# Gate products in 64-row pairs, a 128-row pass for the sines, whole gate blocks in chosen slots, keys four slots ahead

## Chip, cores and metric

The program runs on one core of one Trainium2 chip. The core has five engines with instruction queues of their own: TensorE for matrix products (PE in the profile, its weight loads shown apart as PEld), VectorE (DVE), ScalarE (ACT), GpSimd (POOL) and SyncE (SP, which here only issues DMAs). The metric is the device time of one execution in microseconds (us). Lower is better. Before the change it is 2940.25 us, the median of three runs (2938.42 to 2941.7).

## What is computed

The reference is a block of two layers over x of 8 x 512 x 256 (batch, tokens, width) and a context of the same shape: cross-attention, a feed-forward part, a second cross-attention, a second feed-forward part. Only the first cross-attention is touched. It has 16 heads of 64, and every attention weight is multiplied by a gate that depends on the two tokens' boxes:

```python
delta_x = log(clip(abs((cx_q - cx_k) / w_q), 0.001, None))    # delta_y alike
delta_w = log(w_q / w_k)                                      # delta_h alike
mul = (100.0 * stack([delta_x, delta_y, delta_w, delta_h]))[..., None] * [1, 1000 ** -0.5]
emb = concatenate([sin(mul), cos(mul)])                       # 16 numbers for a pair of tokens
g   = relu(einsum('bnmd,hd->bhnm', emb, Wg) + bg)             # 16 numbers -> 16 heads
a   = q @ k.T / sqrt(64)
mn  = softmax(log(clip(g, 1e-6, None)) + a)
out = (mn @ v) @ Wo.T + bo
```

The softmax over log g + a is computed as g times exp(a), divided by its own sum. All arithmetic is float32.

## The kernel before

**Stages.** First a stage projects keys, values and queries of the eight batches to device memory and prepares the boxes (about the first 356 us). Then comes the loop of the gated cross-attention, to about 1960 us, and after it the attention across the batch, the routed experts and the second layer (the rest). The change lies in the loop and in what the first stage prepares for it.

**The loop.** There are 32 steps (`NSTEP`), one for each batch and each tile of 128 queries. A step has eight slots `p`, one for each pair of heads. In slot `p` of step `i` PE does, in this order: the scores of pair p+1 (`scores`, L469: two products that use 64 rows each, one per head, in two PSUM banks), a piece of the next step's gates (`gate_half`, L449), the eight transposes of the exponentials of pair p (`weigh`, L485), a second piece, the products of pair p-1 with the values (`values`, L505), and in some slots a third piece, the transposes of the output (`outputs`, L527, slots 1, 3, 5, 7) or the output projection (`mix`, L536, slot 2). DVE takes the row maxima of the scores (L473), multiplies the transposed exponentials by the gates (L487) and divides by the sums (L511, L513). ACT takes the exponentials (L476). The order on PE, ACT and DVE is the order of the code (`MANUAL`)[...]. The order of the DMAs on SP is chosen by the scheduler.

**The gates.** For the x and y differences each query has its own sines and cosines over the keys. For width and height the sine of a difference of logs falls apart into products of a query's and a key's numbers, so eight rows (`qx`, `kx`) serve all queries, and a ninth carries the bias. A block of 13 queries (`QB`) so needs 4 x 13 rows of sines, 9 shared rows and 4 x 13 rows of cosines: 116 rows of PE (`GR`), sines from row 0, cosines from row 64. The weights `emb` (116 rows x 128 keys) are loaded, the table `wst` (116 rows x 13 queries x 16 heads) is streamed, and the result has keys as rows. Ten blocks (`NB`) times four groups of 128 keys make 40 products a step. A half block is two key groups in one PSUM bank of 2 x 208 columns; two such banks alternate (tag `g`, `bufs=2`). Each half is copied to the gate tile by one instruction (L455), on DVE in slots 0, 2 and 7, on ACT in the others: 9 and 11 copies a step. The number of halves for each slot is `HALVES`.

**The sines' numbers.** `lt` and `nt` hold 5 passes of 512 keys (`NP`): rows 0 to 51 and 64 to 115 are two blocks of queries. For a step two or three ahead the loop runs `offsets` (DVE, L324, slots 4 and 5), `sizes` (ACT, absolute value, L330, slot 5), `clip` (DVE, slot 6), `log` (ACT, slot 7), `turns` (DVE, next step's slot 0), `whole` and `rest` (DVE, slot 1), `rest_sizes` (DVE) and `sines` (ACT, twice, L352 and L353, slot 2). Four DMAs (`place`, L361, slot 3) then bring `lt` and `nt` to their rows of `emb`. `lt` may be written again by `offsets` once its DMAs have landed.

**Loads.** SP fetches one pair's keys three slots ahead (`load_key`, L419, 3 buffers) and values two ahead (`load_value`, L425, 3 buffers). PSUM [...]: scores 2, transposes 2, gates 2, outputs 2.

## Time and profile before

| what | value |
|---|---|
| median of three runs | 2940.25 us |
| the profiled execution | 2940.68 us |
| its span, first to last instruction | 2938.9 us |
| mean granted TensorE clock | 0.987 of full |
| one step of the loop, mix to mix | 49.75 us, 32 steps |
| DVE busy in a step | 37.4 us |
| ACT busy in a step | 30.3 us |
| DMA in the loop | about 150 GB/s, 0.55 of the 16 engines' time |

The profile has a page with a busy time for each engine, groups of equal instructions with their mean duration, and a timeline. In a timeline line the first number is the start, the second the length of the merged stretch, and "x8" the number of instructions in it. Float32 products go through PE in two passes, and each pass is an instruction of its own in the trace with a weight load in front of it; so 40 gate products are 80 passes. A transpose is one pass. Ends of PE instructions are modelled, so distances between starts are used for PE, not durations.

### The profile page before, as it was taken

The numbers are of one execution on the slowest core, as the hardware profiler recorded it, in microseconds if no ns is written. First come the engines' busy times: TensorE is split into PE (matmuls) and PEld (weight loads), VectorE is DVE, ScalarE is ACT, GpSimd is POOL, SyncE is SP. The second block draws the span as 40 slices with busy tenths as digits, with TensorE's granted clock in tenths as the row PEclk, the third lists the DMA queues.
The fourth block names the chain that finished last, engine by engine and source line by source line (L and its number), as shares of the span: only waits on it lengthen the run. The fifth ranks groups of instructions, "written<-read, shape, count | busy, mean of one in ns | idle before, by whom it ended". The sixth has DMA issues, their size and how long they took to land.

```text
span 2938.9 us, 39143 instructions
## 1 busy us (share of the span) xinstructions
PE 2866.8 (98%) x15188; PEld 2095.2 (71%) x15188; DVE 1826.5 (62%) x2862; ACT 1404.0 (48%) x2196; POOL 138.4 (5%) x138
## 2 busy tenths in 40 slices
PE   8999999999999999999999999999999998999998
PEld 3444478888888888888888888877775665456566
DVE  6432177777777777777777767557862112566757
ACT  4332256566666666656565665435541121343434
POOL 2000000000000000000000000000002111212100
PEclk9999999999999999999999999999998998999999
DMA  7775545555555555454546464443113333111100
GB/s 226 220 227 188 180 119 155 142 155 142 150 152 146 156 140 158 135 163 131 166 131 167 131 166 129 134 128 140 47 55 129 129 127 107 58 44 57 29 15 22
DMA packets 270105, 381.84 MB, mean 130 GB/s; under 512 B 55048, under 2 KB 136840, under 8 KB 267104
## 3 DMA queue, kind: packets, MB, share of 16 engines
q1 hardware_dynamic: 266848, 370.95, 43.9%
q0 software_dynamic: 3072, 8.39, 1.0%
q8 instruction: 120, 1.97, 0.3%
q14 instruction: 65, 0.53, 0.1%
HBM read 237.23 MB, written 73.88 MB: 106 GB/s over the span
## 4 chain that ended last, share of the span: by engine, by line
PE 79%; DVE 13%; issue 2%; DMA 2%; ACT 1%; SPq 0%; POOL 0%; ACTq 0%; DVEq 0%; POOLq 0%
PE pg L449 13%; PE po L505 11%; PE pS L469 7%; PE pT L485 6%; PE pk L226 6%; PE ph L1525 4%; PE pw L536 4%; PE ph L1308 4%; PE py L1317 4%; PE py L1540 4%; PE pv L241 3%; DVE nm L473 2%; PE pz L1497 2%; DVE lt L346 2%; PE pq L700 2%
## 5 line engine op out<-in xcount | busy, mean ns | idle before, releaser
L476 ACT ACTIVATE e<-pS,nm 128x512 f32<-128x512 f32 x512 | 324.3, 684 | 576.4 <-DVE nm L473 576.0
L449 PE MATMUL pg<-wst,emb 116*128 116x208 f32 (+1 forms) x2560 | 581.5, 350 | 8.1 <-DVE gate L455 5.8
L449 PEld LDWEIGHTS pg<-wst,emb 116*128 116x128 f32 x2560 | 414.1, 189 | 205.2 <-issue 79.8
L505 PEld LDWEIGHTS po<-v,at 128*128 128x128 f32 x4096 | 493.0, 192 | 0.1
L505 PE MATMUL po<-v,at 128*128 128x65 f32 x4096 | 485.7, 272 | 0.0
L473 DVE TENSOR_REDUCE nm<-pS 128x2 f32<-128x1024 f32 x256 | 312.5, 1221 | 176.2 <-PE pS L469 176.2
L487 DVE SCALAR_TENSOR_TENSOR at<-gate,pT 128x1024 f32<-128x1024 f32 x256 | 311.1, 1215 | 46.4 <-PE pT L485 45.4
L469 PE MATMUL pS<-kT,qT 64*128 64x512 f32 x1024 | 291.2, 641 | 5.6 <-ACT e L476 2.0
L485 PE MATMUL pT<-ident,e 128*128 128x128 f32 x2048 | 266.4, 273 | 0.0
L485 PEld LDWEIGHTS pT<-ident,e 128*128 128x128 f32 x2048 | 239.8, 141 | 13.9 <-DVE o L513 1.5
L455 DVE COPY gate<-pg 128x416 f32<-128x416 f32 (+1 forms) x289 | 164.6, 570 | 51.2 <-PE pg L449 30.9
L455 ACT COPY gate<-pg 128x416 f32<-128x416 f32 x351 | 166.7, 531 | 33.6 <-PE pg L449 31.2
L1321 DVE TENSOR_TENSOR ye<-py,b 128x256 f32<-128x256 f32 x32 | 13.6, 424 | 208.0 <-PE py L1317 208.0
L1312 ACT ACTIVATE hT<-ph,eb 128x512 f32<-128x512 f32 x64 | 44.0, 687 | 177.7 <-PE ph L1308 171.9
L226 PE MATMUL pk<-ctxT,wk__121 128*128 128x512 f32 x256 | 114.9, 604 | 11.2 <-DMA ctxT<-in_ctxT 7.6
L63 POOL TENSOR_TENSOR ln_rs<-ln_ve,mhalf 128x4 f32<-128x4 f32 (+1 forms) x25 | 25.5, 1019 | 2050.5 <-DVE ln_ve L62 1990.3
L1525 PE MATMUL ph<-xnT,wf 128*128 128x512 f32 (+2 forms) x320 | 118.7, 513 | 1.8 <-ACT xnT L1393 1.5
L536 PE MATMUL pw<-wo,oT 128*128 128x256 f32 x512 | 117.6, 383 | 0.5 <-ACT oT L528 0.5
L241 PE MATMUL pv<-wv,ctxT 128*128 128x512 f32 x256 | 114.7, 593 | 1.0 <-DVE vs L245 1.0
L1308 PE MATMUL ph<-dT,w 128*128 128x512 f32 x256 | 111.9, 595 | 2.7 <-DVE dT L1293 2.1
L469 PEld LDWEIGHTS pS<-kT,qT 64*128 64x128 f32 x1024 | 77.8, 184 | 51.1 <-issue 36.4
L226 PE MATMUL pk<-xnT,wq 128*128 128x512 f32 x256 | 113.0, 594 | 0.6 <-DVE xnT L261 0.6
(252 smaller groups left out, 3910.7 us busy)
## 6 DMA issues: line engine op xcount, KB each, us to landing
v<-vdr SPq DMA_DIRECT2D x256, 260.0 KB
kT<-kdr SPq DMA_DIRECT2D x256, 256.0 KB
emb<-lt SPq DMA_DIRECT2D x64, 520.0 KB
emb<-nt SPq DMA_DIRECT2D x64, 520.0 KB
vdr<-vs SPq DMA_DIRECT2D x8, 2080.0 KB
kdr<-st SPq DMA_DIRECT2D x64, 256.0 KB
qdr<-st SPq DMA_DIRECT2D x64, 256.0 KB
qT<-qdr SPq DMA_DIRECT2D x32, 512.0 KB
```

The source lines that it names most:

```text
L226: nc.tensor.matmul(pk, w[:, c, m * P : (m + 1) * P], src[:, c, :], start=(c == 0), stop=(c == 1))
L449: nc.tensor.matmul(pg[:, c, 0 : nq * H], embs[i % 2][R, blk // 2, blk % 2, kc * P : (kc + 1) * P], wst[i % 2][R, q0 * H : (q0 + nq) * H], ...
L455: copy(gates[i][:, :, 2 * hf : 2 * hf + 2, q0 : q0 + nq].rearrange("p h k q -> p k h q"), pg[:, :, 0 : nq * H].rearrange("p k (q h) -> p k ...
L469: nc.tensor.matmul(pS[:, t, :], qTs[i][rows, p, :], kT[rows, :], start=True, stop=True)
L473: nc.vector.tensor_reduce(nm, pS, AX.X, ALU.max, negate=True)
L476: nc.scalar.activation(e[:, t, :], pS[:, t, :], AF.Exp, bias=nm[:, t : t + 1])
L485: nc.tensor.transpose(pT[:, t, kc, :], e[:, t, kc * P : (kc + 1) * P], ident)
L487: nc.vector.scalar_tensor_tensor(at, gates[i][:, 2 * p : 2 * p + 2], 1e-6, pT, ALU.max, ALU.mult)
L505: nc.tensor.matmul(po[:, 2 * (p % 2) + t, :], at[:, t, kc, :], v[:, kc, t, :], start=(kc == 0), stop=(kc == NQ - 1),)
L536: nc.tensor.matmul(pw, oT[:, c, :], wo[:, c, :], start=(c == 0), stop=(c == PAIRS - 1))
L1308: nc.tensor.matmul(ph, w1[:, c, f * P : (f + 1) * P], dT[:, c, :], start=(c == 0), stop=(c == 1),)
L1525: nc.tensor.matmul(ph[:, 0:n], wf[:, c, f * P : (f + 1) * P], xnT[:, c, tok], start=(c == 0), stop=(c == 1),)
```

## The change

- **Blocks.** The 128 queries of a step are split into two halves of 64 (`HQ`). A block has 6 queries of each half (`QB`), 4 x 6 sines, 4 x 6 cosines and 9 shared rows: 57 rows (`GR`), one half at row 0 and the other at row 64. There are 11 blocks; the last has 4 queries of each half. A product has 57 rows and 96 columns (64 in the last block). `gate_block` issues eight products: for each of four key groups one from rows 0 to 56 and one from rows 64 to 120, into two PSUM banks (tags `g0` and `g1`, one buffer each). Each bank is then copied by one instruction.
- **Slots.** Every slot starts with one block, ahead of the scores. Slots 0, 1 and 5 have a second block between the scores and `weigh`. `BLOCKS` says which engine copies each of the two banks ("A" for ACT, "V" for DVE): 12 copies on ACT and 10 on DVE a step.
- **Sines' numbers.** The rows of `lt` and `nt` are packed without gaps: five groups of 24 rows and one of 8, 128 rows in all, with 4 passes of 512 keys. `offsets` is whole in slot 4, `sizes` in slot 5, `clip` and `log` in slot 6, `turns` in slot 7, `whole` in slot 0, `rest` in slot 1. `place` has ten DMAs for `lt` (slot 3) and ten for `nt` (slot 4). `load_products` and `load_keys` have more DMAs with fewer rows each.
- **Keys** are loaded four slots ahead into four buffers.
- In the first stage `wst` has 128 rows of 64 queries in place of 116 rows of 128, and the steps prepared there follow the new layout.

```diff
-QB = 13
-NB = 10
-GR = 64 + 4 * QB
+HQ = P // 2
+QB = 6
+NB = 11
+GR = 8 * QB + 9
+NS = P // (4 * QB)
...
-        def place(j):
-
-            for src, r0 in ((lt, 0), (nt, 64)):
-                for half in range(2):
+        def place(j, *trig):
+
+            for c in trig or (0, 1):
+                src, r0 = (lt, nt)[c], 4 * QB * c
+                for s in range(NS):
+                    rows = src[4 * QB * s : 4 * QB * (s + 1)]
+                    for g in (s // 2,) if s < 4 else (0, 1):
+                        b0, n = (4 * (s % 2), 4) if s < 4 else (8, 2)
+                        nc.sync.dma_start(
+                            out=embs[j % 2][64 * g + r0 : 64 * g + r0 + 4 * QB, b0 : b0 + n, :],
+                            in_=rows[:, 0:4, :] if s < 4 else rows[:, 2 * g : 2 * g + 2, :],
+                        )
+                for t in range(4):
+                    at = 64 * (t // 2) + r0 + 8 * (t % 2)
                     nc.sync.dma_start(
-                        out=embs[j % 2][r0 : r0 + 4 * QB, :, half, :],
-                        in_=src[64 * half : 64 * half + 4 * QB],
+                        out=embs[j % 2][at : at + 8, NB - 1, :], in_=src[4 * QB * NS :, t, :]
                     )
...
-                kTs[i, p] = wk.tile([P, S], F32, name="kT", tag="kT", bufs=3)
+                kTs[i, p] = wk.tile([P, S], F32, name="kT", tag="kT", bufs=4)
...
+        def gate_block(i, blk, engines="AV"):
...
+            if i == 0 and blk % 2:
+                pT = ps.tile([P, 2, NQ, P], F32, name="pT", tag="t")
+                pgs = [pT[:, g] for g in range(2)]
+            else:
+                pgs = [ps.tile([P, NQ, P], F32, name=f"pg{g}", tag=f"g{g}") for g in range(2)]
+            for kc in range(NQ):
+                for g in range(2):
+                    rows = slice(64 * g, 64 * g + GR)
+                    nc.tensor.matmul(
+                        pgs[g][:, kc, 0 : nq * H],
+                        embs[i % 2][rows, blk, kc * P : (kc + 1) * P],
+                        wst[i % 2][rows, q0 * H : (q0 + nq) * H],
+                        start=True, stop=True,
+                    )
+            for g in range(2):
+                q = HQ * g + q0
+                copy = nc.scalar.copy if engines[g] == "A" else nc.vector.tensor_copy
+                copy(
+                    gates[i][:, :, :, q : q + nq].rearrange("p h k q -> p k h q"),
+                    pgs[g][:, :, 0 : nq * H].rearrange("p k (q h) -> p k h q", h=H),
+                )
...
+        BLOCKS = (("AA", "AV"), ("AA", "AV"), ("AV",), ("VV",), ("AV",), ("AA", "AV"), ("AV",), ("VV",))
...
-                    load_key(i, p + 3)
+                    load_key(i, p + 4)
+                    gate_block(i + 1, next(blocks), BLOCKS[p][0])
                     scores(i, p + 1)
-                    if p == SINES:
+                    if p == 2:
                         features(i + 2, rest_sizes, sines)
-                    if p == LOG:
-                        features(i + 3, log)
-                    half()
+                    if p == 5:
+                        features(i + 3, sizes)
+                    if p == 6:
+                        features(i + 3, clip, log)
+                    for engines in BLOCKS[p][1:]:
+                        gate_block(i + 1, next(blocks), engines)
                     weigh(i, p)
-                    half()
                     values(i, p - 1)
                     load_value(i, p + 2)
-                    half()
...
                     if p == 3:
-                        features(i + 2, load_products, place)
+                        features(i + 2, load_products, lambda j: place(j, 0))
                         load_rest(i)
                     if p == 4:
-                        features(i + 3, lambda j: offsets(j, 0, 3))
-                    if p == 5:
-                        features(i + 3, lambda j: offsets(j, 3, NP), sizes)
-                    if p == 6:
-                        features(i + 3, clip)
+                        features(i + 2, lambda j: place(j, 1))
+                        features(i + 3, lambda j: offsets(j, 0, NP))
+                    if p == 7:
+                        features(i + 3, turns)
```

## Prediction

> **What bounds the kernel now.** I read the page first, then one step of the loop in windows.

> ```profile
> span 2938.9 us, 39143 instructions
> PE 2866.8 (98%) x15188; PEld 2095.2 (71%) x15188; DVE 1826.5 (62%) x2862; ACT 1404.0 (48%) x2196; POOL 138.4 (5%) x138
> ```
> ```profile
> 990.15:1039.90 49.75, 49.58 (x330) 41.29 (x329) 37.39 (x46) 30.31 (x40) 0.00 (x0) 1.00 0.54 150
> ```

> In the window (length, then busy PE, PEld, DVE, ACT, POOL, the clock, DMA share, GB/s) PE is busy for 49.58 of 49.75 us at full clock. A busy PE need not be a PE that can't go faster, so I take starts. A slot with gates (timeline, slot 4), and a slot of the last step, which has none:

> ```profile
> 1048.92 1.13 PE L469 MATMUL pS<-kT,qT 64*128 64x512 f32 x4
> 1049.98 0.97 PE L449 MATMUL pg<-wst,emb 116*128 116x208 f32 x4
> 1050.78 1.04 PE L485 MATMUL pT<-ident,e 128*128 128x128 f32 x8
> 1051.66 0.87 PE L449 MATMUL pg<-wst,emb 116*128 116x208 f32 x4
> 1052.37 1.90 PE L505 MATMUL po<-v,at 128*128 128x65 f32 x16
> 1054.19 1.13 PE L469 MATMUL pS<-kT,qT 64*128 64x512 f32 x4
> ```
> ```profile
> 1943.03 1.13 PE L469 MATMUL pS<-kT,qT 64*128 64x512 f32 x4 [0.50 <-ACT e L476]
> 1944.09 1.09 PE L485 MATMUL pT<-ident,e 128*128 128x128 f32 x8
> 1945.02 1.90 PE L505 MATMUL po<-v,at 128*128 128x65 f32 x16
> 1946.75 0.39 PE L527 MATMUL pt<-ident,o 128*128 128x128 f32 x2
> 1947.07 1.13 PE L469 MATMUL pS<-kT,qT 64*128 64x512 f32 x4
> ```

> Each group starts when the one before has streamed: nothing is waited for but PE. A gate pass costs (1052.37 - 1051.66)/4 = 0.176 us. The first half costs 0.80, 0.1 more, because a weight load stands bare after the change from 64 to 128 rows. Without gates a slot is 1947.07 - 1943.03 less the 0.22 of its two pt transposes: **3.82 us**. In the whole loop the waits list for PE has under 8 us. So the loop is PE's, and a PE saving counts until another engine is late.

> **PE's work.** Removed in a step: 72 passes of 0.176 and 8 narrower ones of 0.15, 13.9 us. Added: 88 products, 176 passes with 96 columns, two at a time if the halves of the rows work together. The nearest row is in the attention across the batch: products of 64 rows and 128 columns that alternate between the two halves of the rows as the new ones do.

> ```profile
> 2052.73 0.71 PE L738 MATMUL pS<-qkT 64*128 64x128 f32 x8
> ...
> 2053.38 1.13 PE L807 MATMUL pw<-ow,oT 128*128 128x256 f32 x4
> ```

> Eight passes take 0.65 us. Of this 0.2 is the change of shape ([...]the four score passes above, two pairs of 0.43, take 1.06, so again 0.2). That leaves 0.45 for four pairs: 0.112 a pair. The po passes, with 65 columns, also come every 0.11, [...]96 columns won't be cheaper. A block is 8 x 0.112 = **0.90 us**, eleven are 9.86.

> [...]the new blocks stand beside the scores, which are 64-row work already, so a slot keeps its two changes; were each block alone, eleven more visits would cost 4.4 us a step. [...] The row has 56 ns per pass[...]. I take the row[...].

> Step after, without waits: 8 x 3.82 + 9.86 + 4 x 0.22 (pt) + 3.45 (pw, 1039.87 to 1043.42[...]) = 44.75. Counting before the same way gives 49.35, so 0.4 is unaccounted for. I carry it: **45.15**, 4.6 less. A single-block slot is 4.7 us, a double one 5.6.

> **New waits: the banks.** Two banks alternated; now each half has one, and a block needs the copies of the block before. Durations for the copies come from these rows, with the DVE and ACT steps of the same slot:

> ```profile
> 1050.16 1.22 DVE L473 TENSOR_REDUCE nm<-pS 128x2 f32<-128x1024 f32 x1 [2.58 <-PE pS L469]
> ...
> 1051.42 1.27 ACT L476 ACTIVATE e<-pS,nm 128x512 f32<-128x512 f32 x2 [1.97 <-DVE nm L473]
> ...
> 1052.58 0.92 ACT L455 COPY gate<-pg 128x416 f32<-128x416 f32 x2
> ...
> 1054.86 1.45 DVE L324 TENSOR_SCALAR lt<-kd,qs,qi 116x512 f32<-116x512 f32 x3
> ```

> Two ACT copies of 416 take 0.92; of 384, 0.87[...]. Runs of 6 in place of 13 I cost at nothing to 0.05 each, and take little: the L455 rows of 416 and 352 on DVE (584 and 520 ns) fall by element.

> Slots 0, 1, 5, from the first weight load: block 1 streams to 0.97, ACT copies run 1.2 to 2.07, the scores end at 1.86. Block 2's second half waits for its bank until 2.1, and its weights load bare: **0.4 us**, three times, 1.2. Both ends: 0.3 and 0.6.

> Slot 6 is worse. In slot 4 DVE runs the maxima, the multiply, L511, L513 (which waits for po, until 5.5) and then four offsets at 0.49: they end 2.6 us into slot 5. The maxima, ready at 2.1, go 2.6 to 3.85; exponentials to 5.15; then `sizes`, 2048 elements, 2.34 - 0.43 = 1.91 us, to 7.0; only then ACT's copy of block 8, to 7.45. Slot 5 with its pt and its 0.4 ends at 6.25, and slot 6 begins with a block that needs this bank: **1.2 us** of wait. PE has no work it may pull ahead. Stalls are 2.4; the step is 47.55, **2.2 less**.

> **Edits that stay beside.** Sines' passes shrink from 2560 to 2048 elements: ACT 4 x 0.43, DVE about 2.1 us a step; neither engine bounds, and their gain is already in the chain above. Table loads stay four. `log` in slot 6 keeps ACT until exponentials of slot 7 end 0.7 into slot 0, scores need their bank at 1.0: 0.3 of cover, lost one for one beyond. Sines after slot 2 lie beside the 3.45 of pw. Keys four ahead remove the 1.2 us in all that PE waited for kT; but they must outlast the 20 place DMAs and two or four of products on SP in place of 4 and one or two.

> SP is the doubtful part:

> ```profile
> 992.34 0.86 SPq L361 DMA_DIRECT2D emb<-lt  x1
> 994.75 0.32 SPq L544 DMA_DIRECT2D x1q<-xo  x1
> 995.13 1.40 SPq L361 DMA_DIRECT2D emb<-lt  x1
> 999.05 0.32 SPq L425 DMA_DIRECT2D v<-vdr  x1
> ```

> Today lt's two DMAs are out by 996.5, and the offsets start at 1005.1 with no wait. Ten DMAs at 0.35 to 0.45 need about 4 us; bytes are the same 1.04 MB, at the 150 to 200 GB/s of the loop 5 to 7 us. If the scheduler puts v, which waits for po at the end of slot 3, ahead of some of them, they are issued about 13 to 16.5 us after slot 2 began and land by 18 to 20.5. The offsets come at 18.6. So their wait is 0 to 2 us; I take 0, and every us of it is one more at slot 6.

> Before the loop: gates for step 0, 14.1 us of passes to 9.9, less 4; the extra DMAs on SP and the larger memset on POOL cost 0 to 3 beside PE's projections, taken as 0. The tail is untouched.

> **Sum.** 31 steps compute gates: 31 x 2.2 = 68, and 4: 2940.7 (the profiled execution; the median is 2940.25, 0.4 lower) - 72 = **2868 us**. Its own range, stalls 1.5 to 3.3: 2840 to 2896. Chance 0.48.

> **Rivals.**
> - *Hardly any stall*: copies free the banks in time, 0.9 a step. For it: ACT is busy only 30.3 of 49.75. Against: order, not load, delays the copy. 31 x 3.7 + 4: 2822. Chance 0.13.
> - *The sines' numbers land 1.5 us late*: 31 x 0.7 + 4, 2915. Chance 0.16.
> - *They land 4 us late* (slower): DVE stands at the offsets in slot 4, behind them the maxima of slot 5, the exponentials, `sizes`, the copy, and PE in slot 6. Stalls 6.4, 31 x 1.8 - 4: 2993. It decides from 2.3 us late, a landing 21 us after slot 2 began. For it: twenty small DMAs in one queue that also waits for po. Against: the 3.7 us that lt's landing (1001.4) has in hand today. Chance 0.15.
> - *PE can't be fed* at 28 ns an instruction[...]. Chance 0.05.
> - *The pairs don't overlap* (the change doesn't do what it says): 88 x 2 x 0.112 = 19.7 a step, 31 x 5.3 and 6 before the loop: 3110. L738 speaks against it. Chance 0.03.

> **Range.** 2808 to 2955 takes in the first four of these outcomes but for their edges, and leaves out most of the last three slow ones; some 0.2 is outside. What can be told from no change is 0.2%, 6 us. Faster 0.77 (forecast, small stalls, most of 1.5 late, the feeding), same 0.04, slower 0.19.

> **What would show it.** Pair passes 0.112 apart in blocks of 0.9; steps of 47 to 48 us; PE waits at the gate product for ACT's copy, near 0.4 in slots 0, 1, 5 and near 1.2 at slot 6, about 2.4 in a step; offsets without a wait for emb's DMAs. Steps at 45.5 mean no stall, above 49.75 the slower rival, and then DVE must show a wait for a DMA before L324's successor. Passes 0.2 apart would make the forecast wrong at its root.

## The result: 1.8% slower

| | before | after |
|---|---|---|
| median, side by side | 2939.69 us (2938.42 to 2941.7) | 2993.89 us (2987.94 to 2997.47) |
| ratio, with its 95% interval | | 1.0182 (1.0164 to 1.0199) |
| mean granted clock, profiled execution | 0.987 | 0.954 |
| start of the first gate product | 356.0 us | 367.5 us |
| from there to the first mix (pw) | 86.9 us | 89.3 us |
| first mix to last mix, the loop | 1514.5 us | 1558.4 us |
| last mix to the end | 981.5 us | 976.6 us |

So 43.9 us were lost in the loop and 13.9 ahead of its first mix. The end, which the change does not touch, gave 5 back; but it varies from 973 to 984 us between the versions below, so nothing can be read from these 5. The page of the changed kernel (its first line, the engines' busy times, the granted clock in 40 slices, and two groups of instructions):

```profile
span 2991.7 us, 46273 instructions
...
PE 2814.4 (94%) x18260; PEld 2057.7 (69%) x18260; DVE 1767.1 (59%) x2862; ACT 1366.5 (46%) x2228; POOL 139.1 (5%) x137
...
PEclk9999989999999999899999999999998999899999
...
L470 PE MATMUL pg<-wst,emb 57*128 57x96 f32 (+1 forms) x5552 | 436.4, 293 | 105.9 <-ACT gate L479 105.0
...
L331 DVE TENSOR_SCALAR lt<-kd,qs,qi 128x512 f32<-128x512 f32 x128 | 61.7, 543 | 92.6 <-DMA emb<-lt 74.1
```

PE is no longer always busy (94% in place of 98%). The last column of a group is the idle time just ahead of it: PE stands for 105 us ahead of the gate products until ACT has copied, and DVE for 74 us ahead of the offsets until the DMAs have read `lt`. The list of waits, from 500 to 1900 us, gives the same pair for the loop alone (sum, times, longest):

```profile
PE pg L470 <- ACT gate L479: 99.4, 27, 6.1
DVE lt L331 <- DMA emb<-lt: 65.5, 25, 5.0
```

One wait of 4.43 us, followed back. The timeline of the changed kernel, slots 4 to 6 of a step whose slot 2 began at 1117.48 (SP, DVE, ACT, PE, one below the other):

```profile
1130.51 0.34 SPq L441 DMA_DIRECT2D v<-vdr  x1
1130.95 5.37 SPq L372 DMA_DIRECT2D emb<-lt  x6
1136.36 2.71 SPq L378 DMA_DIRECT2D emb<-lt  x4
...
1135.67 0.42 DVE L537 TENSOR_TENSOR o<-po,rec 128x256 f32<-128x256 f32 x1
1139.40 1.92 DVE L331 TENSOR_SCALAR lt<-kd,qs,qi 128x512 f32<-128x512 f32 x4 [3.30 <-DMA emb<-lt]
1141.23 1.22 DVE L497 TENSOR_REDUCE nm<-pS 128x2 f32<-128x1024 f32 x1
...
1142.48 1.26 ACT L500 ACTIVATE e<-pS,nm 128x512 f32<-128x512 f32 x2 [5.11 <-DVE nm L497]
1143.64 1.91 ACT L337 ACTIVATE lt<-lt 128x2048 f32<-128x2048 f32 x1
1145.44 0.48 ACT L479 COPY gate<-pg 128x384 f32<-128x384 f32 x1
...
1141.15 0.39 PE L551 MATMUL pt<-ident,o 128*128 128x128 f32 x2
1145.97 2.03 PE L470 MATMUL pg<-wst,emb 57*128 57x96 f32 x16 [4.43 <-ACT gate L479]
1147.79 1.97 PE L493 MATMUL pS<-kT,qT 64*128 64x512 f32 x4
```

Read it from the top. The value load is held until slot 3 is over, and the ten DMAs of `lt` stand behind it. They take 8.1 us to issue (1130.95 to 1139.07). DVE has been free for the offsets since 1136.1 and starts them at 1139.40. Behind them, in the order of the code, come the maxima, the exponentials, `sizes` and only then the copy that frees PE's bank. And PE then runs slowly: the block takes 1.8 us and the scores 1.9, about twice their usual 0.97 and 0.98. The windows of the same kernel show why (length, busy times, then the clock):

```profile
1026.60:1074.20 47.60, 45.69 (x427) 38.33 (x425) 35.36 (x46) 29.14 (x41) 0.00 (x0) 1.00 0.54 155
1145.60:1152.40 6.80, 6.43 (x33) 4.93 (x34) 3.08 (x4) 2.36 (x5) 0.00 (x0) 0.50 0.62 172
```

The clock is halved for 6.8 us, from just before the end of the wait. The loop has 25 such windows, 167 us in all; the loop of the kernel before has none. The other step shown, of 47.6 us, kept its clock; DVE waited 0.78 there, because two of the ten DMAs had left ahead of the value load. In two steps of four all ten leave behind the value load, and these steps last 52 to 55 us.

The first stage has a wait of the same kind. The timeline of the changed kernel there:

```profile
142.25 1.51 SPq L372 DMA_DIRECT2D emb<-lt  x2
143.81 2.67 SPq L378 DMA_DIRECT2D emb<-lt  x4
146.52 4.84 SPq L372 DMA_DIRECT2D emb<-nt  x6
151.41 2.67 SPq L378 DMA_DIRECT2D emb<-nt  x4
...
171.64 1.91 ACT L359 ACTIVATE lt<-lt 128x2048 f32<-128x2048 f32 x1 [7.92 <-DVE nt L84]
...
174.18 6.40 PE L228 MATMUL pk<-xnT,wq 128*128 128x512 f32 x8 [3.93 <-ACT st L232]
```

Sixteen of the twenty DMAs for one step's sines' numbers follow one another on SP and hold it for 12 us. Afterwards ACT stands for 7.9 us at a sine, ahead of the bias copies that PE's banks wait for, and PE's next eight products take 6.4 us in place of 3.6.

### The profile page after: what moved, and what is told of

Same layout as the page of the kernel before. It is cut to its first block, busy times and chain, and to the rows that moved or that the text cites. A ratio compares the mean times of both kernels' runs of the same rounds, so it can differ in the third digit from the quotient of the medians.

```text
span 2991.7 us, 46273 instructions
## 1 busy us (share of the span) xinstructions
PE 2814.4 (94%) x18260; PEld 2057.7 (69%) x18260; DVE 1767.1 (59%) x2862; ACT 1366.5 (46%) x2228; POOL 139.1 (5%) x137
## 4 chain that ended last, share of the span: by engine, by line
PE 74%; SPq 5%; ACT 4%; DVE 3%; DMA 3%; issue 1%; POOL 0%; ACTq 0%; DVEq 0%; POOLq 0%
PE po L529 12%; PE pg L470 11%; PE pT L509 7%; PE pS L493 7%; PE ph L1541 4%; PE pw L560 4%; PE ph L1324 4%; PE py L1333 4%; PE py L1556 4%; SPq L372 3%; PE pk L228 3%; PE pz L1513 2%; ACT lt L337 2%; PE pq L716 2%; PE pS L1490 2%; SPq L378 1%
## 5 line engine op out<-in xcount | busy, mean ns | idle before, releaser
L470 PE MATMUL pg<-wst,emb 57*128 57x96 f32 (+1 forms) x5552 | 436.4, 293 | 105.9 <-ACT gate L479 105.0
L470 PEld LDWEIGHTS pg<-wst,emb 57*128 57x128 f32 x5552 | 391.8, 199 | 196.0 <-ACT gate L479 154.9
L529 PE MATMUL po<-v,at 128*128 128x65 f32 x4096 | 493.8, 274 | 0.0
L511 DVE SCALAR_TENSOR_TENSOR at<-gate,pT 128x1024 f32<-128x1024 f32 x256 | 310.8, 1214 | 26.9 <-PE pT L509 26.8
L509 PE MATMUL pT<-ident,e 128*128 128x128 f32 x2048 | 297.2, 291 | 0.0
L479 DVE COPY gate<-pg 128x384 f32<-128x384 f32 (+1 forms) x316 | 160.9, 525 | 202.3 <-PE pg L470 180.1
L479 ACT COPY gate<-pg 128x384 f32<-128x384 f32 x378 | 174.8, 488 | 200.9 <-PE pg L470 196.9
L247 DVE TENSOR_TENSOR vs<-pv,bv 128x512 f32<-128x512 f32 x64 | 43.9, 689 | 135.6 <-PE pv L243 135.6
L331 DVE TENSOR_SCALAR lt<-kd,qs,qi 128x512 f32<-128x512 f32 x128 | 61.7, 543 | 92.6 <-DMA emb<-lt 74.1
```

Source lines behind the costliest of these rows:

```text
L470: nc.tensor.matmul(pgs[g][:, kc, 0 : nq * H], embs[i % 2][rows, blk, kc * P : (kc + 1) * P], wst[i % 2][rows, q0 * H : (q0 + nq) * H], sta ...
L479: copy(gates[i][:, :, :, q : q + nq].rearrange("p h k q -> p k h q"), pgs[g][:, :, 0 : nq * H].rearrange("p k (q h) -> p k h q", h=H),)
L509: nc.tensor.transpose(pT[:, t, kc, :], e[:, t, kc * P : (kc + 1) * P], ident)
L511: nc.vector.scalar_tensor_tensor(at, gates[i][:, 2 * p : 2 * p + 2], 1e-6, pT, ALU.max, ALU.mult)
L529: nc.tensor.matmul(po[:, 2 * (p % 2) + t, :], at[:, t, kc, :], v[:, kc, t, :], start=(kc == 0), stop=(kc == NQ - 1),)
```

## The experiments

The theory: the ten DMAs of `lt` take twice the time that was counted, the offsets wait for them, and DVE, ACT and PE are chained behind the offsets; a wait of PE then costs more than its length, because half clock goes with it. All ratios are against the kernel before, with 95% intervals. Two parts of the chain were cut first, one alone, the other alone, and both.

**The DMAs of `lt` ahead of the mix.**

```diff
                     if p == 2:
+                        features(i + 2, load_products, lambda j: place(j, 0))
                         mix(i - 1)
                     if p == 3:
-                        features(i + 2, load_products, lambda j: place(j, 0))
                         load_rest(i)
```

> Only change to the changed kernel: the ten DMAs of lt (and the loads of the products) stand in slot 2 of the code, ahead of the value load of slot 3, so that SP issues them as soon as the sines are there. Landing theory (the offsets on DVE wait for lt's landing because SP holds its DMAs behind a value load, and this wait is handed on through maxima, exponentials, absolute values and ACT's copy to PE): the offsets' wait falls from 65 us in all to under 10, PE's longest wait at the gate product from 6.1 to about 1.3 us, the loop loses 65 us and some or all of the half-clock windows (another 0 to 68 us): 2858 to 2926 us. Bank theory (the stall comes from one buffer for each bank and the order of ACT's queue, whatever DMA lands when): PE still waits 2 to 5 us in each step, 2980 to 2995. Array theory (the clock falls because 57-row pairs count as little work): the waits go but the half-clock windows stay, one in a step, about 2926.

Measured: 2877.44 us, ratio 0.9793 (0.9777 to 0.9809). (`load_products`, at most four DMAs, moves along.) The timeline of this kernel, the same place in a step:

```profile
1122.35 5.04 SPq L372 DMA_DIRECT2D emb<-lt  x6
1127.43 3.02 SPq L378 DMA_DIRECT2D emb<-lt  x4
...
1132.96 1.91 DVE L331 TENSOR_SCALAR lt<-kd,qs,qi 128x512 f32<-128x512 f32 x4
...
1139.53 1.57 PE L470 MATMUL pg<-wst,emb 57*128 57x96 f32 x16 [1.03 <-ACT gate L479]
```

The ten DMAs take their 8.1 us as before, but end 2.5 us before the offsets are due. The offsets wait for nothing, and what is left at slot 6 is the 1.0 to 1.2 us that the prediction had there. So 116 us hung on the place of ten DMAs in SP's queue. Steps are 46.76 us, or 48.4 where a window of half clock follows; there are 13 such windows, of 3.4 us.

**The copy that PE waits for, on DVE.** In slot 5 the first half of block 8 is copied by DVE, so that it no longer stands behind `sizes` on ACT.

```diff
-        BLOCKS = (..., ("AV",), ("AA", "AV"), ("AV",), ("VV",))
+        BLOCKS = (..., ("AV",), ("AA", "VV"), ("AV",), ("VV",))
```

> Only change to the changed kernel: both banks of slot 5's second block are copied by DVE, none by ACT, so the absolute values on ACT no longer stand between the late offsets and PE. Landing theory: the offsets still wait about 65 us in all, but PE's wait at slot 6 is shorter by 2.3 us in every step (exponentials 1.3, absolute values 1.9, ACT's copy 0.5, against one more DVE copy 0.5 and the overlap): 2.2 us gaps vanish, 4.5 to 6 us gaps become 2.2 to 3.5. Most half-clock windows go: 2870 to 2920 us. Bank theory with DVE as the late copier: waits move to DVE's copies and stay as long, 2980 to 3000. Array theory: 60 us less from the waits, clock unchanged, about 2930.

Measured: 2895.44 us, ratio 0.9866 (0.9848 to 0.9883). The list of waits of this kernel, 500 to 1900 us:

```profile
DVE lt L331 <- DMA emb<-lt: 57.9, 21, 4.6
...
PE pg L470 <- DVE gate L479: 26.4, 14, 3.1
```

DVE waits for the landing nearly as long as in the changed kernel, 57.9 us, but PE waits 26.4 in place of 99.4. So 98 us hung on the chain behind the landing (exponentials and `sizes` in front of a copy). The late landing still costs without it: 69 us against the version with both edits, which differs from this one in the place of the DMAs alone. Half clock goes with these waits too, 65 us of it in the loop.

**Both edits.**

> Both edits together. Landing theory: no wait over 0.6 us for a bank anywhere, steps of 45.7 us as in the one step of the changed kernel that has no offsets, clock 1.0 through the loop: 28 steps x (51.6 - 45.7) = 167 us less than 2994, 2825 us, faster than the kernel before. Array theory: the half-clock window in each step stays and takes 2 to 3.4 us: 2890 to 2920. Bank theory: above 2950.

Measured: 2826.34 us, ratio 0.9633 (0.9611 to 0.9655). The full steps are 45.65 to 45.68 us but for one of 45.94, and the windows view from 500 to 1000 us shows no idle PE and no lost clock:

```profile
500.00:1000.00 500.00, 499.81 (x4648) 420.05 (x4649) 390.75 (x504) 316.42 (x428) 0.00 (x0) 1.00 0.61 165
```

The gate products and the number of copies are those of the slower kernel; one copy has changed its engine. What made that kernel slower in the loop was the order of ten DMAs and the place of this one copy.

**The first stage's DMAs on another queue.** In the changed kernel, the sines' numbers of the first two steps are placed through POOL's queue, not SP's.

```diff
...
-                    features(j, whole, rest, rest_sizes, sines, place)
+                    features(j, whole, rest, rest_sizes, sines, lambda j: place(j, queue=nc.gpsimd))
```

> Only change to the changed kernel: the forty DMAs that place the sines' numbers of the first two steps, ahead of the loop, are issued from POOL's queue and not from SP's. Theory for the first stage (SP is held for 12 to 14 us at a time by these DMAs while the stores of keys and queries wait behind them, so ACT's buffers fill and PE stands): the projections end near 355 us as before and not at 366.6: 10 to 12 us less, 2982. Rival (the stage is longer for other reasons, such as the half-clock windows at 172 and 261 us arising from the work's own order): no change within 3 us.

Measured: 2993.94 us, ratio 1.0202 (1.0179 to 1.0225), and the last product of the projections starts at 367.9 us (366.0 in the changed kernel; this start is meant below where the projections "end"). No gain: POOL now waits 10 us for the sines ahead of these DMAs, and a step of the normalization in POOL's queue, which waits 17 us for DVE, holds up twelve of the twenty. So this run does not tell what the DMAs cost on SP, and three more asked it.

**No such DMAs in the first stage**, in the version with both edits: `place` is left out of the same line.

> The version with both edits (2826.34 us), and in the first stage the DMAs that place the sines' and cosines' numbers of the first two steps left out (their features enter the gates of steps 0 and 1 as zeros; everything else is computed). Theory S (two blocks of twenty such DMAs, 12 to 14 us each on SP's queue, hold up the offsets of the next step, the loads and the stores behind them, and with these ACT and PE): the projections end at 354 to 357 us, as in the kernel before (354.5), in place of 364 to 366, the two windows of half clock ahead of 300 us are gone, and the time is about 2815 to 2818. Rival A (the features' steps stand at another place in ACT's order and wait there for DVE, whatever SP does): the projections still end at 363 to 366, and the time is 2824 to 2829.

Measured: 2816.18 us, ratio 0.9595 (0.9572 to 0.9617). The projections end at 354.4 us in place of 365.3, and both windows of half clock ahead of 300 us are gone (one of 3.4 us, at 111 us, is new). Rival A falls: ACT's order alone did not do it. (The half clock at step 0 is still there, now 27.3 us.)

**No features of the first two steps at all.**

> The same version, but all of the features of the first two steps left out of the first stage, their work on DVE and ACT as well as their DMAs (the gates of steps 0 and 1 lack them; step 2's are kept). Theory S and rival A both: the projections end at 352 to 356 us and the time is 2812 to 2818. If they still end at 363 to 366, the 11 us come from neither, but from what else the change does in this stage: twelve key loads in place of four, tables of 128 rows, the larger memset.

Measured: 2807.37 us, ratio 0.9562 (0.9546 to 0.9579); the projections end at 349.6. What is left of the change in this stage (tables, key loads, the memset) does not show: 349.6 is below the 354.5 of the kernel before. The features' work on DVE and ACT costs some 5 us in the place that it has there.

**The same work, spread.** Nothing is left out. Offsets in batches 1, 4, 7, sines in 2, 5, and the twenty DMAs in two tens, one batch apart.

```diff
+                j = b // 3
+                if b in (3, 6):
+                    place(j - 1, 0)
+                if b in (4, 7):
+                    place(j - 1, 1)
-                if b in (1, 3, 5):
-                    j = b // 2
+                if b in (1, 4, 7):
                     offsets(j, 0, NP)
                     features(j, sizes, clip, log, turns)
-                if b in (2, 4):
-                    j = b // 2 - 1
+                if b in (2, 5):
                     load_products(j)
-                    features(j, whole, rest, rest_sizes, sines, place)
+                    features(j, whole, rest, rest_sizes, sines)
```

> The version with both edits (2826.34 us), with the first stage's features spread: offsets in batches 1, 4, 7, sines in 2, 5, their ten DMAs in 3, 6 and the cosines' ten in 4, 7, so that no offsets stand right behind the twenty DMAs and no block on SP is over some 7 us. Theory S (the block of twenty on SP and what stands behind it made the 11 us of the first stage): the projections end at 354 to 358 us, and the time is 2813 to 2820 with nothing left out. Rival (any twenty such DMAs there cost this much, wherever they stand): 362 to 366, 2824 to 2830.

Measured: **2809.71 us**, ratio 0.9561 (0.9543 to 0.9579), the fastest of all that do the whole work. The projections end at 348.7, earlier than expected and earlier than before the change (354.5). SP in the timeline of this kernel:

```profile
141.23 0.75 SPq L372 DMA_DIRECT2D emb<-lt  x1
142.56 5.47 SPq L237 DMA_DIRECT2D kdr<-st  x4
148.08 0.74 SPq L372 DMA_DIRECT2D emb<-lt  x1
149.43 3.75 SPq L237 DMA_DIRECT2D kdr<-st  x3
```

The DMAs now go out between the stores, singly or up to seven in a row, which hold SP for 5 us at most; in the version with both edits the longest rows are 16 and 19 DMAs, 12 and 14.5 us. They are as many as before. The work on DVE and ACT has moved to other batches too, so this run does not say which of the two moves gave how much.

**Work added where PE waits.** Ahead of slot 6 the changed kernel gets products that nobody reads, in the bank of the second half, which is free before that of the first.

```diff
+        def warm(n):
+            pg = ps.tile([P, NQ, P], F32, name="pg1", tag="g1")
+            for _ in range(n):
+                nc.tensor.matmul(pg[:, 0:2, :]..., ident, wo[:, 0, :], start=True, stop=True)
...
+                    if p == 6 and i + 1 < NSTEP:
+                        warm(12 if i % NQ in (2, 3) else 4)
                     gate_block(i + 1, next(blocks), BLOCKS[p][0])
```

> The changed kernel (2993.89 us) with work added and nothing removed: ahead of the first gate block of slot 6, where PE waits, twelve products of 128 rows by 256 columns into the bank of the second half (four in the steps where the wait is short). Theory C (a wait of PE costs twice, since the clock is halved for 3.4 or 6.8 us after it: 25 windows, 167 us long, in the loop): PE's idle time there falls from 2.0 and 4.5 us to 1 to 1.7 us, the windows of half clock in the loop fall to 50 to 90 us, and the time falls by 40 to 60 us, to 2935 to 2955. Rival W (only the waiting counts, and the clock falls for another reason, such as the pair passes themselves): 2992 to 3015, the added products costing nothing or up to 0.7 us a step.

Measured: 2990.42 us, ratio 1.0179 (1.0162 to 1.0196): no gain, though the half clock in the loop fell from 167 us to 44. The timeline of this kernel says why:

```profile
1147.30 7.13 PE L487 MATMUL pg<-wo,ident 128*128 128x256 f32 x24 [1.72 <-DVE gate L479]
1154.37 1.15 PE L470 MATMUL pg<-wst,emb 57*128 57x96 f32 x15
```

Twelve products are 24 passes. They took 7.1 us, and ended about 4 us after ACT had freed the bank (1150.3). The clock that was won went into that. The time lies outside both ranges, and the run decides nothing; it was repeated in a smaller size, `warm(4 if i % NQ in (2, 3) else 2)`.

> The added products again, but fewer: four ahead of slot 6 in the steps with the long wait and two in the others (a product took 0.59 us in the run with twelve, so 2.4 and 1.2 us; the bank that they use is free 1.4 us after PE has come to stand, the other 3.0 us after that). Theory C (a wait of PE costs twice, by the half clock after it): the added products end before the bank for the gates is free, the windows of half clock in the loop fall from 167 us to 40 to 90, and the time falls from 2993.89 to 2930 to 2955. Rival W (the clock after the wait does not decide): 2988 to 3000, as with twelve.

Measured: 2943.96 us (2934.95 to 2962.48), ratio 1.0016 (1.0004 to 1.0028): 50 us off the changed kernel, by adding work. The timeline of this kernel:

```profile
1117.80 0.39 PE L559 MATMUL pt<-ident,o 128*128 128x128 f32 x2
1119.80 1.99 PE L487 MATMUL pg<-wo,ident 128*128 128x256 f32 x8 [1.61 <-DVE gate L479]
1122.80 1.14 PE L470 MATMUL pg<-wst,emb 57*128 57x96 f32 x16 [1.01 <-ACT gate L479]
1123.77 1.05 PE L501 MATMUL pS<-kT,qT 64*128 64x512 f32 x4
```

The wait of 4.6 us is still there, cut into 1.6, two of products and 1.0, and the block behind it streams in 0.97. Windows of half clock in the loop: 44 us in place of 167, while DVE's wait for the landing stayed (63.8 us). Over the 28 steps PE's idle time fell by 51 us, and the products took about 43 of them; the half clock cost 46 us less. So the second price of a wait, the clock, is shown apart from the first.

**Keys three slots ahead**, in the version with both edits: `bufs=3` and `load_key(i, p + 3)`.

> The version with both edits (2826.34 us), with the keys loaded three slots ahead from three buffers, as in the kernel before. Theory N (three slots are enough: the longest block on SP is some 8 us, 1.7 slots, and a key loaded three slots ahead is needed two slots later): PE's wait for kT stays under 6 us in all, 2824 to 2832. Rival K (four slots are needed beside twenty DMAs): PE waits for kT in each step for 1 us or more, the clock falls after it, and the time is 2870 to 2930.

Measured: 2860.7 us, ratio 0.9744 (0.9727 to 0.9761), 34 us more than with four, between the two ranges. The list of waits, 500 to 1900 us:

```profile
PEld pS L493 <- issue: 18.7, 33, 1.7
PE pS L493 <- DMA kT<-kdr: 11.5, 19, 1.6
```

With four slots the first of these rows reads 1.0 us and the second does not appear. Beside blocks of 8 us on SP, three slots are too few. The wait is under the 1 us a step of rival K, but there.

**The same products, one half after the other**, in the version with both edits.

```diff
-            for kc in range(NQ):
-                for g in range(2):
+            for g in range(2):
+                for kc in range(NQ):
```

> The version with both edits (2826.34 us), with the same products in another order: all passes of a block in one half of the rows, then all of the other half, in place of alternating. Theory P (two passes run at the same time only where neighbours in the order are in different halves): passes come 0.107 to 0.112 us apart, a block takes 1.7 to 1.8 us in place of 0.90, a step 54.5 to 55.6 in place of 45.66, and the time is 3090 to 3140. Rival O (the pace does not depend on the order, only on the columns or the instruction): 2824 to 2835.

Measured: 2943.06 us in one run, steps of 49.31 us. Between both theories: alternating is worth 3.65 us a step, some two fifths of what theory P said. A block in the timeline of this kernel:

```profile
1117.83 1.32 PE L470 MATMUL pg<-wst,emb 57*128 57x96 f32 x13
1118.88 0.69 PE L493 MATMUL pS<-kT,qT 64*128 64x512 f32 x1
1118.99 0.50 PE L470 MATMUL pg<-wst,emb 57*128 57x96 f32 x3
1119.32 1.05 PE L493 MATMUL pS<-kT,qT 64*128 64x512 f32 x3
```

Sixteen passes one after another at 0.112 would take 1.79. In the records behind these lines each half keeps 0.112 between its passes, but the second half starts at 1118.35, 0.53 after the first, when three of the first half's eight are still to come; and the scores start at 1118.88, ahead of the last three passes of the second half. The halves overlap in part, then: here passes started ahead of three that stand before them in the code and use the other half of the rows. Still, without alternation the version with both edits stands about where the old kernel stood (2939.93 beside it).

**Full rows beside the pairs of step 0**, in the version with both edits: one product of 128 rows into bank `m` behind each gate block of step 0.

> The version with both edits (2826.34 us), with one product of all 128 rows by 256 columns added behind each gate block of step 0 (eleven, 0.3 to 0.6 us each). Theory R (a stretch of nothing but pair passes does not bring the halved clock back[...]; full rows do): the window of half clock from 370 us, 20.5 us long there, falls to 3.4 to 10.2 us; the time is within 6 us, since the products cost what the clock brings. Rival T (the clock comes back after its time, whatever runs): the window stays at 17 to 27 us, and the time is 3 to 8 us longer.

Measured: 2840.85 us, ratio 0.9668 (0.9647 to 0.9688), 14.5 us more. The windows view:

```profile
370.00:404.00 34.00, 30.84 (x185) 22.11 (x186) 6.66 (x12) 7.71 (x14) 0.00 (x0) 0.58 0.29 100
```

From 372.1 the clock is halved for 27.3 us (20.5 without the added products, but 27.3 in three other versions without them). From the first gate product to the first mix it takes 98.8 us in place of 88.7; the rest of the 14.5 us lies in the end, which varies. Theory R falls in the form that was expected: one full-row product behind each block, over a third of the time there, does not bring the clock back. A larger share was not tried. In all thirteen kernels with the new blocks this half clock ended only after the first scores of step 0 had begun (3.0 to 18.5 us after); whether gate passes alone hold it at half is not shown.

## Why the prediction was wrong

**The step that failed** is "Ten DMAs at 0.35 to 0.45 need about 4 us", and with it "So their wait is 0 to 2 us; I take 0". The ten took 8.1 us. The start was right (13.5 us after slot 2 began, where the text had 13), and so was the time at which the offsets are due (18.6). But the last DMA was out at 21.6 and landed at 21.9, past the 20.5 of the text and past the 21 from which its slower rival was to decide. A nearer price stood in the rows that the prediction itself showed: 0.86 and 1.40 us for an `emb<-lt`. The 0.35 to 0.45 belong to the loads from device memory next to it. At 0.8 each, the same working gives a wait of 2.4 us and the time of the landing in the bad steps. Measured: 65.5 us in 25 waits, the longest 5.0.

**The term that was missing** is the clock. The sum paid for each us of waiting once. In the loop the 28 whole steps with offsets took 1445.8 us; at 46.85 (a step of 45.65 without waits, and slot 6's 1.2) they would take 1311.8. Of the 134 between, 65.5 are the landing, and the other 68 are what the half clock took. This is a difference, but it can be had from the trace as well: PE was busy in 135.4 of the 167.3 us of half clock, and half of that is 67.7. The added products confirm it too, by 46 of their 50 us.

**The first stage**, taken as −4 and 0 to 3, cost 13.9 us up to the first mix. SP's extra DMAs did not stay beside PE: 11 us hung on them (the run without them). And the gates of step 0, whose passes shrank as counted, ran at half clock for 20.5 us, behind a wait for a bank of 2.45 us (1.25 before), so that their saving of 4 us was not seen.

**What held.**
- The pair pass of 0.112 us, the block of 0.90 and the step: 45.65 us were measured without offsets, against 45.15 and the bank waits. Those of slots 0, 1 and 5 were too dear in the sum: by the difference 0.5 us for the three, not 1.2.
- Slot 6: 1.2 us forecast, by the chain of offsets, maxima, exponentials, `sizes` and copy; 1.03 of idle PE and a step 1.1 longer in the run that has no late landing.
- Instructions at 28 ns each: no sign of PE starving in steps of 45.66 (PE busy for 499.81 of 500 us in the version with both edits).
- The slower rival, "they land 4 us late", had the mechanism, the place and the chain. That its 2993 us was also the time is half chance: the landing was 2.3 us late a step on average, and the clock paid for the rest.
- Pairs that don't overlap (3110 us): wrong, and its price was too high. Even one after the other, the halves overlap in part.

In sum, against 2868: about 114 us in the loop (134 less 20 for the cheaper banks) and 18 ahead of it, less 5 at the end, 127; measured, 126. The range reached to 2955. It had left out the clock, without which the late landing alone would have stayed inside.

## What to carry to other kernels

Price a DMA by rows with the same source and destination: here moves inside SBUF cost the queue about twice what loads from device memory do (medians of 0.64 to 0.76 us against 0.29 to 0.43), ten of them in a row held it for 8 us and nineteen for 14.6, and such a block needs a place. Where a full PE is the bound, look for the one instruction whose lateness reaches it through other engines' order; moving either end of that chain (ten DMAs, one copy) turned a loss of 1.8% into gains of 2.1% and 1.3%, and both with a spread first stage into one of 4.4%. And count more for a wait of PE than its length: here waits of 1.9 to 6.1 us cost another 2.4 us of clock on average (67.7 us over 28), and waits of 1.03 us another 1.6 in 13 steps of 28.

## What the runs showed of the hardware

```profile
372.00:387.70 15.70, 15.70 (x144) 15.70 (x145) 5.36 (x10) 4.18 (x9) 0.00 (x0) 0.50 0.55 194
```

- **Issue on SP.** A move inside SBUF took 0.76 us (median) with 24 rows of two or four passes and 0.64 with 8 rows of one; a load of keys or values, of 128 rows, 0.32 to 0.43 (medians). Few rows are not the reason: the loads of 4 to 12 rows from device memory (`wst<-qxd`, `emb<-kxd`, `kd<-kcd`) took 0.29 to 0.36 (medians). Nor does the cost follow the bytes much, 0.64 us for 16 KB and 0.76 for up to 196 KB.
- **Passes in different halves of the rows overlapped.** Where they alternate, a pair came every 0.112 us (median); where they do not, the overlap was three passes: with the halves in turn, the second half of a block starts 0.53 us after the first.
